# An attention block in fp32 on one core: the first chunk's transposes on TensorE, the local mask added on VectorE, and a new order of the first loads

## The chip, the core and the metric

The kernel runs on one core of a Trainium2 chip. The core has five engines that each work through a queue of their own in order: TensorE (PE; matmuls, and PEld, its weight loads), VectorE (DVE), ScalarE (ACT), GpSimd (POOL) and SyncE (SP, which here only issues transfers). The engines wait for each other by semaphores. Transfers between DRAM and the core's SBUF memory are issued from the queues of SP and ACT and carried out by 16 DMA engines. Matmuls write to PSUM, a small memory[...].

The metric is the device time of one execution in microseconds (us), lower is better.

## What is computed

The input x has 4 sequences of 1024 tokens with 512 features. After a layer norm (xn) two branches are added to x: an attention and a small product with an 8-bit rounding. The attention has 16 heads of 128 features:

```python
q  = apply_rope(rmsnorm(heads(xn @ Wq + bq), qn_w), pos)
lk = apply_rope(rmsnorm(heads(xn @ Wlk + blk), kn_w), pos)     # local keys
lv = heads(xn @ Wlv + blv)                                     # local values
# sparse part: groups of 4 tokens become one "entry" (softmax weights from xn @ Wcmp + bcmp)
entries = sum over 4 tokens of w_cmp * xn
ck, cv  = apply_rope(rmsnorm(entries @ Wk + bk, kn_w), ends), entries @ Wv + bv
sc = where(entry ended before the token, q . ck * scale, NEG); keep the 8 largest; softmax; times cv
# local part: windows of 128; a token sees the 128 tokens before it and itself
sl = where(0 <= distance <= 128, q . lk * scale, NEG); softmax; times lv
out = (sparse + local) * 0.5 @ Wo + bo
result = x + out + round8(xn * s) @ round8(input2 * s1) / (s * s1)
```

All of it is fp32, but for the 8-bit branch and some constants that are exact in bf16.

## The kernel before

**Tiles.** A chunk is 128 tokens (32 chunks, 8 to a sequence), a unit is one pair of heads of one chunk: 256 units, n = 8 x chunk + pair. All weights stay in SBUF: wqk_sb[u] (the pair's columns of Wq and Wlk, 1 MB), wlv_sb[u] (0.5 MB), wo_sb[u] (0.5 MB). wkv_sb holds Wk, Wv and the column of Wcmp.

**The loop** (L752) is a software pipeline over s from -2 to 257. In iteration s, in the order of the code, TensorE gets: scores of unit s, queries and keys of unit s+2 (`queries`), the output product of unit s-2 (`to_output`), the values of unit s+1 (`values_of`), and the weighted sum of unit s-1 (`values`). Between them `steps()` advances generators that prepare a chunk (`chunk_prep`: norm, transposes, entries) or do its 8-bit branch (`chunk_eight`). There is no planner: under `manual_schedule` each engine's queue has the order in which the code emits, and waits are put in for data and for buffers.

**A unit's way.** `queries` (L437) makes q and lk of both heads in one PSUM tile, qp. ScalarE sums squares (`square_sum`), GpSimd makes 1/rms (r), VectorE scales by it (`normalize`), VectorE and GpSimd rotate. q and k are then token by feature, and the scores need them feature by token. [...] `turn_keys` (L477) turns the blocks (two instructions into thb), SP writes them to DRAM in four transfers (qk), and `fetch_keys` (L497) reads them back in two (qT, lkT), in an order that completes the transpose.

**Scores** (`scores`, L537), for each head: a matmul of a bf16 identity with mask_b puts the local mask (0 or -1e30) into the PSUM columns of the window (L545), q with the previous chunk's keys and with its own adds to it (L547 and L554; a sequence's first chunk has no previous one, and a window of 128 columns), then q with the entries (L557) and a small mask for the last 32 of them (L558).

**Softmax.** `weigh` (L567): VectorE takes the negated maximum of the window (L579, a reduce), the 8 largest of the entries (L580) and replaces them by a mark (L583), ScalarE takes the exponentials with the sum (L584, L587). `settle` and `settle_window` divide by the sums; the result is prob.

**Weights.** They must be turned as well: `turn` (L621) in blocks on VectorE (L628), one write to DRAM (pr) and four reads back (`fetch`, L657; probT). The very last unit has no iteration behind it to hide that in, and uses `turn_last` (L639): TensorE transposes into PSUM (tiles of the tag pp), and one copy each on ScalarE and VectorE to probT.

**Buffers that matter:** PSUM tags qp (2 buffers), sc (2), pp (2, shared by values, transposes and the chunk generators), ctx and out (1 each); SBUF th, thb, probB and probT have one buffer each, lkT has ten.

**The start.** SP loads in this order: x of chunk 0, wqk_0, x of chunk 1, angles, wlv_0, Wk, Wv, Wcmp, wqk_1, angles, wlv_1, wqk_2, wlv_2. ScalarE's queue loads biases and small constants, and its first own work, the copy of chunk 0's transposed xn, stands behind those issues. Ahead of the loop the generator of chunk 0 runs up to "B3", which puts the entries' first matmuls (yp, L349) on TensorE ahead of the first queries. Later weights are loaded from ScalarE's queue at the ends of iterations -2 to 7 (L799 to L804).

Of the kernel before, what the change touches and what calls it, by code (L numbers as in the profile page):

```python
# [19 lines left out]
P = 128  # L20
D = 128
# [17 lines left out]
def kernel(  # L39
# [32 lines left out]
    NE = P // RATIO  # L72
    NT = B * NCH
    assert S // RATIO <= 2 * P and NU == 8 and HID == 512

# [59 lines left out]
    load_angles(0)  # L135
    load_wlv(0, nc.sync)

    wkv_sb = const.tile([P, KK, 2 * D + 1], F32, name="wkv_sb")
    nc.sync.dma_start(wkv_sb[:, :, 0:D], Wk.rearrange("(k p) n -> p k n", p=P))
    nc.sync.dma_start(wkv_sb[:, :, D : 2 * D], Wv.rearrange("(k p) n -> p k n", p=P))  # L140
    with nc.allow_non_contiguous_dma(reason="512 words once"):
        nc.sync.dma_start(
            wkv_sb[:, :, 2 * D : 2 * D + 1], Wcmp.rearrange("(k p) o -> p k o", p=P)
        )
    load_wqk(1, nc.sync)
# [4 lines left out]


    bias_f = work.tile([P, 1024], F32, tag="probT", name="bias_f", bufs=1)[0:BLK, 0:512]
    nc.vector.memset(bias_f, 0.0)
# [304 lines left out]
    def normalize(n):  # L458
# [16 lines left out]
        w["th"], w["thb"] = th, thb  # L475

    def turn_keys(n):  # L477

        w = units[n]
        th = w.pop("th").rearrange("p g (b i) -> p b g i", i=BLK)  # L480
        thb = w.pop("thb")

        nc.vector.transpose(
            thb[:, :, 0, :].rearrange("p b (i g) -> p b g i", g=2), th[:, :, 0:2, :]
        )
        nc.vector.transpose(
            thb[:, :, 1, :].rearrange("p b (g i) -> p b g i", g=2), th[:, :, 2:4, :]
        )
        turned = dram.tile([NB, NB, BLK, 4 * BLK], F32, tag="qk", name=f"qk_{n}")
        for a in range(NB):  # L490
            nc.sync.dma_start(  # L491
                turned[a].rearrange("b j x -> j b x"),
                thb[ds(a * BLK, BLK)].rearrange("p b t x -> p b (t x)"),
            )
        w["turned"] = turned

    def fetch_keys(n):  # L497
        w = units[n]
        turned = w.pop("turned").rearrange("a b j (t x) -> t (b j) a x", t=2)
        qT = work.tile([P, NB, 2 * BLK], F32, tag="qT", name=f"qT_{n}")  # L500
        lkT = work.tile([P, NB, 2 * BLK], F32, tag="lkT", name=f"lkT_{n}", bufs=NU + 2)
        nc.sync.dma_start(qT, turned[0])
        nc.sync.dma_start(lkT, turned[1])
        w["qT"], w["lkT"] = qT.rearrange("p a (i g) -> p (a i) g", g=2), lkT

# [31 lines left out]
    def scores(n, h):  # L537
# [6 lines left out]
        q = qT[:, :, h]  # L544
        nc.tensor.matmul(sc[:, loc], ident_b, mask_b[:, loc], start=True, stop=False)  # L545
        if c:
# [3 lines left out]
                units[n - NU]["lkT"][:, :, ds(h * BLK, BLK)],  # L550
                start=False,
                stop=False,
            )
        nc.tensor.matmul(  # L554
            blocks(sc[:, P : 2 * P]), q, lkT[:, :, ds(h * BLK, BLK)], start=False, stop=True
        )
# [10 lines left out]
    def weigh(n, h):  # L567
# [8 lines left out]
        if n % (NU * NCH) == 0:  # L576

            nc.gpsimd.memset(prob[:, 2 * P + NE : 4 * P], 0.0)
        nc.vector.reduce_max(neg[:, 0:1], sc[:, loc], AX.X, negate=True)  # L579
        nc.vector.max(top, sc[:, spa])  # L580
# [3 lines left out]
        nc.scalar.activation(  # L584
            prob[:, loc], sc[:, loc], AF.Exp, bias=neg[:, 0:1], accum_out=tot[:, 0:1]
        )
# [51 lines left out]

    def turn_last(n):  # L639

        parts = parts_of(n)
        g = len(parts)
        probT = work.tile([P, 1024], F32, tag="probT", name=f"probT_{n}", bufs=1)
        probT = of_heads(probT, n)
        for h in range(2):
            prob = heads.pop((n, h))["prob"]
            tp = pp(f"tp_{n}_{h}")
            for i in range(g):
                nc.tensor.transpose(tp[:, ts(i, P)], prob[:, ts(parts[i], P)], ident)
            copy = nc.vector.tensor_copy if h else nc.scalar.copy  # L650
            copy(
                probT[:, :, ds(h * g, g), :],
                tp[:, 0 : g * P].rearrange("p (g a i) -> p a g i", a=NB, i=BLK),
            )
        units[n]["probT"] = probT

# [67 lines left out]

    NN = NT * NU
    running = []
# [21 lines left out]
    pick_tokens()  # L748
    until(first, "B3")
    masks()  # L750

    for s in range(-2, NN + 2):  # L752
# [12 lines left out]
        for_unit(s, (weigh, 0), (weigh, 1))  # L765
        for_unit(s + 2, (queries,))
        for_unit(s, (settle, 0), (settle, 1))
        if s < 0:
            until(first, "A5" if s == -2 else "B6")
        steps()  # L770
        for_unit(s + 2, (squares, (0, 1, 2, 3)), (spread,))
        for_unit(s, (settle_window, 0), (settle_window, 1))
        for_unit(s - 2, (to_output,))
        steps()
        if s < NN - 1:
            for_unit(s, (turn,))
        if s == -1:
            until(first, "B7")
        for_unit(s + 1, (values_of,))
        if s == -1:  # L780
            until(first, "B8")
        for_unit(s + 2, (normalize,))
        for_unit(s - 1, (values,))
        if s < NN - 1:
            for_unit(s, (fetch,))
        else:
            for_unit(s, (turn_last,))
        for_unit(s + 2, (turn_keys,), (fetch_keys,))
        for_unit(s + 1, (keep_values,))
# [64 lines left out]
```

## Time and profile before

| | |
|---|---|
| Median of 3 runs | 2868.39 us (2865.25 to 2873.09) |
| The profiled execution | 2864.43 us, of which the traced span is 2862.7 us |
| TensorE busy | 2812.8 us (98%), 13417 matmuls |
| VectorE busy | 2209.7 us (77%) |
| ScalarE busy | 1300.8 us (45%) |
| GpSimd busy | 816.8 us (29%) |
| DMA | 408.25 MB, mean 143 GB/s |
| Granted TensorE clock, mean | 0.995 |

How to read it: a group's line gives the source line, engine, operation, output<-input by tile names, shapes and count; then busy time in us, the mean of one in ns, and the idle time of the engine ahead of it with what ended it. In the timeline a line is: start (us), duration (us), engine, line, operation, tiles, shape, how many were merged, and in brackets the idle time before it and its releaser. An fp32 matmul appears as two instructions (x2 for one product). Matmuls are pipelined, so that recorded durations overlap, and differences of starts tell how long one holds the engine. A row of the window table has: the window, its length, busy time and count for PE, PEld, DVE, ACT and POOL, then the granted clock, the DMA share and GB/s. The row of digits for PE is its busy share in tenths, in 40 equal slices of the span.

### The profile page before, as it was taken

To read this page: it belongs to the slowest core of one execution; us is meant where nothing else is said; L and a number is where in the kernel's file an instruction comes from. 1 tells how busy PE (TensorE), PEld (TensorE's weight loads), DVE (VectorE), ACT (ScalarE), POOL (GpSimd) and SP (SyncE) were. 2 spreads that over 40 slices of the span, in tenths; PEclk is the share of its full clock that TensorE was granted. 3 is DMA by queue.
4 is the path that set the end of the run, shared out by engine and by line. 5 is a ranking of instruction groups with operands and counts; after the bars stand their busy time and mean duration, and the time that the engine had idled before them with its cause. 6 is when DMAs were issued, how large, how long until landed. Compare 5 with 4: busy or idle time off the path is not lost. (4 is left out here: it accounts for less than half of the span.)

```text
span 2862.7 us, 48785 instructions
## 1 busy us (share of the span) xinstructions
PE 2812.8 (98%) x13417; PEld 1903.9 (67%) x13417; DVE 2209.7 (77%) x8636; ACT 1300.8 (45%) x5059; POOL 816.8 (29%) x1161
## 2 busy tenths in 40 slices
PE   6899999999999999999999999999999999999998
PEld 3566666666666666666666666666666666666766
DVE  5677778888777777788877777777887777787786
ACT  2344444444444444444444444444444444444443
POOL 3433222322233232222222332322223223322221
PEclk8999999999999999999999999999999999999999
DMA  7644445555444445555444444555554445455554
GB/s 240 169 138 134 130 136 151 149 151 144 137 124 132 136 133 143 147 150 150 145 132 124 138 131 131 152 147 146 146 150 126 131 126 139 131 151 148 145 146 123
DMA packets 639665, 408.25 MB, mean 143 GB/s; under 512 B 316480, under 2 KB 591776, under 8 KB 639392
## 3 DMA queue, kind: packets, MB, share of 16 engines
q1 hardware_dynamic: 627696, 391.57, 48.4%
q10 hardware_dynamic: 11696, 13.56, 1.5%
q8 instruction: 107, 1.75, 0.3%
q14 instruction: 166, 1.36, 0.2%
HBM read 216.72 MB, written 188.22 MB: 141 GB/s over the span
## 5 line engine op out<-in xcount | busy, mean ns | idle before, releaser
L442 PE MATMUL qp<-wqk,xnT 128*128 128x512 f32 x2048 | 947.5, 605 | 0.0
L442 PEld LDWEIGHTS qp<-wqk,xnT 128*128 128x128 f32 x2048 | 371.7, 192 | 381.3 <-issue 371.0
L584 ACT ACTIVATE prob<-sc,neg 128x256 f32<-128x256 f32 (+1 forms) x512 | 236.1, 461 | 626.5 <-DVE taken L583 601.1
L511 PEld LDWEIGHTS vp<-wlv,xnT 128*128 128x128 f32 x2048 | 389.0, 190 | 161.1 <-issue 112.7
L712 PE MATMUL op<-wo,cT 128*128 128x512 f32 x1024 | 488.0, 599 | 0.6 <-ACT cT L694 0.5
L511 PE MATMUL vp<-wlv,xnT 128*128 128x256 f32 x2048 | 483.8, 379 | 0.0
L628 DVE STREAM_TRANSPOSE probB<-prob 128x512 f32<-128x512 f32 (+2 forms) x510 | 289.1, 604 | 143.4 <-ACT prob L610 136.2
L293 ACT ACTIVATE junk<-qp 128x128 bf16<-128x128 f32 x1024 | 284.3, 278 | 247.8 <-PE qp L443 212.1
L523 ACT COPY lv<-vp 128x256 f32<-128x256 f32 x256 | 95.3, 372 | 515.0 <-PE cp L679 442.1
L306 POOL TENSOR_TENSOR rb<-th,cs 128x256 f32<-128x256 f32 x256 | 247.2, 966 | 279.3 <-DVE th L464 279.1
L287 POOL TENSOR_SCALAR r<-ss 128x4 f32<-128x4 f32 x256 | 49.5, 193 | 935.5 <-ACT junk L293 930.3
L712 PEld LDWEIGHTS op<-wo,cT 128*128 128x128 f32 x1024 | 186.6, 190 | 179.3 <-issue 128.9
L464 DVE SCALAR_TENSOR_TENSOR th<-qp,r,norm_w 128x128 f32<-128x128 f32 x1024 | 282.8, 338 | 27.4 <-POOL r L288 26.9
L679 PE MATMUL cp<-probT,lv 128*128 128x128 f32 x1920 | 297.9, 275 | 3.4 <-DMA probT<-pr 3.4
L679 PEld LDWEIGHTS cp<-probT,lv 128*128 128x128 f32 x1920 | 275.2, 192 | 18.2 <-issue 5.1
L288 POOL TENSOR_TENSOR r<-r,nhalf 128x4 f32<-128x4 f32 x256 | 259.7, 1014 | 21.4
L679 PE MATMUL cp<-probT,cv 128*128 128x128 f32 x1536 | 255.6, 275 | 0.0
L554 PE MATMUL sc<-lkT,qT 128*128 128x128 f32 x1024 | 210.7, 288 | 21.5 <-DMA lkT<-qk 21.4
L557 PE MATMUL sc<-ckT,qT 128*128 128x96 f32 (+7 forms) x1024 | 226.9, 303 | 0.0
L610 ACT ACTIVATE prob<-prob,tot 128x256 f32<-128x256 f32 (+1 forms) x512 | 222.8, 484 | 2.9 <-DVE tot L604 2.9
L679 PEld LDWEIGHTS cp<-probT,cv 128*128 128x128 f32 x1536 | 213.1, 192 | 0.0
L308 DVE TENSOR_TENSOR th<-thb,rb 128x128 f32<-128x128 f32 x256 | 87.2, 341 | 158.6 <-POOL rb L306 158.6
(120 smaller groups left out, 4143.1 us busy)
## 6 DMA issues: line engine op xcount, KB each, us to landing
qk<-thb SPq DMA_DIRECT2D x1024, 64.0 KB, 2.0
pr<-probB SPq DMA_DIRECT2D x127, 512.0 KB, 2.6
probT<-pr SPq DMA_DIRECT2D x508, 128.0 KB, 2.9
pr<-probB SPq DMA_DIRECT2D x96, 384.0 KB, 2.3
probT<-pr SPq DMA_DIRECT2D x384, 96.0 KB, 2.4
qT<-qk SPq DMA_DIRECT2D x256, 128.0 KB, 2.3
lkT<-qk SPq DMA_DIRECT2D x256, 128.0 KB, 2.5
x_norm<-_attn_hidden_states_dram SPq DMA_DIRECT2D x32, 256.0 KB, 3.2
```

The lines of the kernel that those rows point to most:

```text
L288: nc.gpsimd.tensor_tensor(r, r, nhalf[: ss.shape[0], 0:n], ALU.pow)
L293: nc.scalar.activation(junk[: src.shape[0]], src, AF.Square, accum_out=acc)
L306: nc.gpsimd.tensor_tensor(bb, x12, wide(cs[:, HALF:ROPE]), ALU.mult)
L442: nc.tensor.matmul(qp, xnT[:, k, :], wqk_sb[u][:, k, :], start=(k == 0), stop=False)
L464: nc.vector.scalar_tensor_tensor(th[:, i, :], qp[:, ts(i, D)], r[:, i : i + 1], norm_w[:, i // 2, :], ALU.mult, ALU.mult,)
L511: nc.tensor.matmul(vp[:, 0:256], xnT[:, k, :], wlv_sb[u][:, k, :], start=(k == 0), stop=(k == KK - 1),)
L557: nc.tensor.matmul(sc[:, spa], q, ckT[:, 0:m], start=True, stop=False)
L584: nc.scalar.activation(prob[:, loc], sc[:, loc], AF.Exp, bias=neg[:, 0:1], accum_out=tot[:, 0:1])
L610: nc.scalar.mul(prob[:, loc], prob[:, loc], tot[:, 0:1])
L628: nc.vector.transpose(pb[:, :, ds(h * g, g), :], prob[:, parts[0] * P : (parts[-1] + 1) * P].rearrange("p (g b i) -> p b g i", b=NB, i=BLK),)
L679: nc.tensor.matmul(blocks(cp[:, h, :]), v, probT[:, :, h * len(parts) + i - parts[0], :], start=(i == parts[0]), stop=(i == parts[-1]),)
L712: nc.tensor.matmul(op, cT[:, h, :], wo_sb[u][:, h, :], start=(u == 0 and h == 0), stop=(u == NU - 1 and h == 1),)
```

## The change

Three things are edited together.

1. **Transposes of the first chunk's units (n = 0 to 7) on TensorE.** `by_dma(n)` tells which units still take the way through DRAM: 8 to 254. For the others q and k are turned by four TensorE transposes into one pp tile (`turn_keys_here`, put behind the queries of the following unit) and copied by ScalarE (qT) and VectorE (lkT) in `keep_keys`. Their softmax weights are turned as in the old `turn_last`, now split into `turn_here` (transposes, put behind `values_of`) and `keep_turned` (the two copies, put where `fetch` stood). With two parts to a head (a first chunk) both heads share one pp tile. The last unit's weights take this way as before, but their transposes now stand ahead of `values` of the unit before.
2. **The local mask on VectorE.** The matmul L545 goes. In `weigh` the reduce is replaced by one fused instruction, which writes -(score + mask) back to the window's PSUM columns and returns their minimum, which is the negated maximum; the exponential then takes scale -1.
3. **The start.** wlv_0 is loaded after Wk and Wv, Wcmp from the head of ScalarE's queue in place of SP's. The generator of chunk 0 no longer runs to "B3" ahead of the loop: yp follows the first queries, and the entries' next matmul (ep) moves from iteration -2 to -1.

```diff
-    load_wlv(0, nc.sync)
     wkv_sb = const.tile([P, KK, 2 * D + 1], F32, name="wkv_sb")
     nc.sync.dma_start(wkv_sb[:, :, 0:D], Wk.rearrange("(k p) n -> p k n", p=P))
     nc.sync.dma_start(wkv_sb[:, :, D : 2 * D], Wv.rearrange("(k p) n -> p k n", p=P))
-        nc.sync.dma_start(wkv_sb[:, :, 2 * D : 2 * D + 1], Wcmp ...)
+    load_wlv(0, nc.sync)
...
+        nc.scalar.dma_start(wkv_sb[:, :, 2 * D : 2 * D + 1], Wcmp ...)
     bias_f = ...
...
+    def by_dma(n):
+        return NU <= n < NN - 1
+    def turn_keys_here(n):
+        w = units[n]
+        th = w.pop("th")
+        w.pop("thb")
+        w["tq"] = tq = pp(f"tq_{n}")
+        for i in range(4):
+            nc.tensor.transpose(tq[:, ts(i, P)], th[:, i, :], ident)
+    def keep_keys(n):
+        w = units[n]
+        tq = w.pop("tq").rearrange("p (t g a i) -> p t g a i", t=2, g=2, a=NB)
+        qT, lkT = key_tiles(n)
+        nc.scalar.copy(qT.rearrange("p a (i g) -> p g a i", g=2), tq[:, 0])
+        nc.vector.tensor_copy(lkT.rearrange("p a (g i) -> p g a i", g=2), tq[:, 1])
...
-        nc.tensor.matmul(sc[:, loc], ident_b, mask_b[:, loc], start=True, stop=False)
...
-        nc.vector.reduce_max(neg[:, 0:1], sc[:, loc], AX.X, negate=True)
+        nc.vector.tensor_tensor_reduce(
+            sc[:, loc], sc[:, loc], mask_b[:, loc], -1.0, TAKEN, ALU.add, ALU.min, neg[:, 0:1]
+        )
...
             prob[:, loc], sc[:, loc], AF.Exp, bias=neg[:, 0:1],
+            scale=-1.0,
             accum_out=tot[:, 0:1],
...
-    def turn_last(n):
+    def turn_here(n):
+        w, parts = units[n], parts_of(n)
         g = len(parts)
+        w["tp"] = []
+        for h in range(2):
+            prob = heads.pop((n, h))["prob"]
+            if h and g == 2:
+                tp = tp[:, g * P :]
+            else:
+                tp = pp(f"tp_{n}_{h}")
+            for i in range(g):
+                nc.tensor.transpose(tp[:, ts(i, P)], prob[:, ts(parts[i], P)], ident)
+            w["tp"].append(tp[:, 0 : g * P])
+    def keep_turned(n):
...
-    until(first, "B3")
     masks()
     for s in range(-2, NN + 2):
...
         for_unit(s + 2, (queries,))
+        if not by_dma(s + 1) and s < NU:
+            for_unit(s + 1, (turn_keys_here,))
         for_unit(s, (settle, 0), (settle, 1))
         if s < 0:
-            until(first, "A5" if s == -2 else "B6")
+            until(first, "B4" if s == -2 else "B6")
         steps()
         for_unit(s + 2, (squares, (0, 1, 2, 3)), (spread,))
+        if not by_dma(s + 1) and s < NU:
+            for_unit(s + 1, (keep_keys,))
         for_unit(s, (settle_window, 0), (settle_window, 1))
...
-        if s < NN - 1:
-            for_unit(s, (turn,))
+        if by_dma(s):
+            turn(s)
...
         for_unit(s + 1, (values_of,))
+        if not by_dma(s):
+            for_unit(s, (turn_here,))
         for_unit(s + 2, (normalize,))
         for_unit(s - 1, (values,))
-        if s < NN - 1:
-            for_unit(s, (fetch,))
+        if by_dma(s):
+            fetch(s)
         else:
-            for_unit(s, (turn_last,))
-        for_unit(s + 2, (turn_keys,), (fetch_keys,))
+            for_unit(s, (keep_turned,))
+        if s + 2 >= NU:
+            for_unit(s + 2, (turn_keys,), (fetch_keys,))
```

## The prediction

> **What bounds the kernel now.** I read the page first, then the stretches by window, then one unit in the timeline, then the list of waits. The page gives TensorE 98% of the span and a row of nines; the window table shows where the other 2% is:
>
> ```profile
> PE 2812.8 (98%) x13417; PEld 1903.9 (67%) x13417; DVE 2209.7 (77%) x8636; ACT 1300.8 (45%) x5059; POOL 816.8 (29%) x1161
> PE   6899999999999999999999999999999999999998
> 0.00:40.00 40.00, 18.78 (x56) 11.39 (x57) 16.99 (x64) 6.46 (x25) 9.74 (x30) 0.91 0.76 224
> 40.00:80.00 40.00, 27.76 (x107) 17.46 (x105) 25.82 (x98) 12.04 (x56) 16.01 (x19) 0.84 0.84 257
> 80.00:120.00 40.00, 34.82 (x145) 21.68 (x146) 27.86 (x121) 15.47 (x68) 21.46 (x25) 0.90 0.61 173
> 120.00:160.00 40.00, 39.83 (x187) 26.27 (x186) 27.98 (x124) 17.94 (x74) 9.42 (x14) 1.00 0.51 142
> ```
>
> So there are two kernels: the first 120 us, where TensorE is idle for 38.6 us (120 - 18.78 - 27.76 - 34.82) and its granted clock (the column after POOL) falls to 0.84 to 0.91; and 2,740 us in which it never stops. What it waits for in the first part is in the timeline, first at the loads, then at the keys on their way through DRAM:
>
> ```profile
> 15.41 3.76 PE L349 MATMUL yp<-wkv_sb,xnT 128*128 128x257 f32 x8 [8.00 <-DMA wkv_sb<-in_L_attn_Wcmp_dram]
> 38.47 6.08 PE L442 MATMUL qp<-wqk,xnT 128*128 128x512 f32 x8
> 52.56 0.77 PE L554 MATMUL sc<-lkT,qT 128*128 128x128 f32 x2 [5.57 <-DMA lkT<-qk]
> 82.45 0.79 PE L554 MATMUL sc<-lkT,qT 128*128 128x128 f32 x2 [7.64 <-DMA lkT<-qk]
> ```
>
> Eight queries matmuls take 6.08 us there and 3.68 us later: after a long wait TensorE also runs slow. In the steady part the order of starts tells what an instruction really costs; durations overlap and don't:
>
> ```profile
> 1599.78 0.61 PE L679 MATMUL cp<-probT,lv 128*128 128x128 f32 x4
> 1600.45 0.27 PE L545 MATMUL sc<-mask_b,ident_b 128*128 128x256 bf16 x1
> 1600.56 0.40 PE L547 MATMUL sc<-lkT,qT 128*128 128x128 f32 x2
> 1600.79 0.40 PE L554 MATMUL sc<-lkT,qT 128*128 128x128 f32 x2
> 1601.21 0.18 PE L558 MATMUL sc<-mask_b,ident_b 128*128 128x32 bf16 x1
> 1601.24 0.27 PE L545 MATMUL sc<-mask_b,ident_b 128*128 128x256 bf16 x1
> 1601.35 0.40 PE L547 MATMUL sc<-lkT,qT 128*128 128x128 f32 x2
> 1602.00 0.18 PE L558 MATMUL sc<-mask_b,ident_b 128*128 128x32 bf16 x1
> 1602.03 3.68 PE L442 MATMUL qp<-wqk,xnT 128*128 128x512 f32 x8
> 1605.55 0.38 PE L443 MATMUL qp<-bias_b,sel 128*128 128x512 bf16 x1
> 1605.76 1.88 PE L712 MATMUL op<-wo,cT 128*128 128x512 f32 x4
> ```
>
> The mask matmul L545 holds TensorE 0.11 us (1600.45 to 1600.56), L558 0.03. Vector's side:
>
> ```profile
> L579 DVE TENSOR_REDUCE neg<-sc 128x1 f32<-128x256 f32 x448 | 180.0, 402 | 8.8 <-PE sc L558 8.4
> L721 DVE TENSOR_TENSOR x_sum<-x_sum,op 128x512 f32<-128x512 f32 x32 | 22.0, 688 | 62.4 <-PE op L712 62.4
> L594 DVE DVE_READ_ACCUMULATOR prob<-taken,prob 128x1 f32 x512 | 42.4, 83 | 0.0
> ```
>
> [...] after L558 (0.03 us) the eight L442 take 3.52 us, not 8 x 0.43 = 3.44 as four L712 (1.72 us) would have it, so 0.08 + 0.03 = 0.11 us of fp32 weight load lie open behind the short matmul. [...] here four L339 transposes, warm, take 0.44 us in all (44.60 to 45.04), so I use 0.11 each. [...]
>
> **The mask off TensorE, 256 units.** For each head L545 goes. First head of a unit: it stood behind a 0.11 us matmul (L679), which will hide the next weight load just as well: 0.11 us saved. Second head: it stood behind L558 and covered the 0.11 us load of the query weights; without it the load starts at L558 and only L558's 0.03 us covers it. Saved: 0.03. Together 0.14 us a unit (0.137 with unrounded starts), whether the mask had 256 or 128 columns. Bounds: 0.06 if the first head's load is exposed too, 0.22 if none is. Units 8 to 255: 248 x 0.137 = 34.0 us.
>
> **The mask on Vector, 512 instructions.** The fused add, negate and minimum reads PSUM and SBUF, writes PSUM and reads out an accumulator; the trace has no such row. Below: the plain reduce's 0.40. Nearest row: L721 less 256 elements at 1.03 ns (L579's 402 at 256 against 270 at 128) is 0.42, the three-operand L427 (750) is 0.49 in the same way, plus 0.08 for the accumulator: 0.50 to 0.57. Above: 1.0, if the unknown form takes two passes. I take 0.57, that is 0.35 us more a unit. What hides it: Vector works 8.6 us of a unit's 11 (2209.7/256), and the turning of the weights (L628) waits for ScalarE's L610 (136.2 us in all, 0.53 a unit), which is behind the squares of this iteration's queries and not behind Vector; a further wait of 0.3 us for r follows it in chunks without earlier window. Without that cover it would delay the next keys by 0.35 a unit.
>
> **What is late next.** Keys of unit n leave in iteration n-2 and must land by n. From the last query matmul to the landing of lkT takes 14.7 us in a first chunk of a sequence (1512.05 to 1526.8), and two units less the 4.8 us of scores and queries leave 2 x 9.9 - 4.8 = 15.0: the 0.3 to spare is what two shorter units take (0.27), and landings vary by more. I count none of the 0.137 there: 24 units of sequences 2 to 4 give back 3.3 us. In second chunks I find lkT landing -0.5 to 2.4 us ahead of the scores, half under 0.3: half of 32 x 0.137, 2.2 us, is given back. Later chunks have 1 to 3 us ahead; 1.9 us for scattered waits. Kept: 34.0 - 7.4 = 26.6 us.
>
> **First chunk and start.** Added: eight transposes a unit, 8 x 0.11 = 0.87 us of TensorE, and two ScalarE and two Vector copies of about 0.4 (L523: 372 ns). Removed: Vector's four block transposes (1.6 us), all of SP's issues for q, k and weights (1 + 4 + 4 + 2 a unit), the wait for the keys. Loads: Wcmp's issue (0.51) moves from SP to the head of ScalarE's queue, where eleven issues and the first copy (ended 10.05) stand behind it: that copy moves to 10.5, and the queue's biases land behind its 512 small packets (bias_b was ready at 11.5, its first use moves to 15.6). wlv (0.5 MB) moves behind Wk and Wv. The entries' first matmuls move behind queries(0).
> Ends of scores, before: 38.5, 54.4, 64.8, 84.3, 95.9, 106.9, 118.1, 127.9 for units 0 to 7. After, step by step: queries(0) from 10.5, wqk_0 having landed at 7.1, half of them at the slow clock: 15.9. Entries' matmuls 1.7: 17.7. queries(1), whose weights land at about 18: 21.8. ScalarE copies y and takes its exponentials first, so squares(0) starts at 19.5, and norm and rotation end 5.65 us later as before: 25.15. TensorE waits 3.4 us for them, turns the keys: 25.7. Entries: ep 26.1, kv 26.9, squares 27.7, unit 1's squares 29.3, GpSimd's r 30.6 (ahead of the entries' rotation in its queue), rotation 31.0, ckT 32.0, scores(0) end 32.8. queries(2), slow clock again as before, 6.1: 38.9; turned keys, one more transpose group and values, 41.5; weights turned once ScalarE's L610 has passed, 42.45; scores(1) end 43.4. From then on a unit is TensorE's own sum: scores 0.92, queries 3.73, keys 0.44, output 1.72, values 1.73, weights 0.44, context 0.89 = 9.87, plus the chunk work of an iteration (0.55, 0.86, 0.17): 53.3, 63.2, 73.6, 83.5, 94.2, 104.3. ScalarE's and Vector's halves end within that (ScalarE's L610 at 6.7 us of the unit, weights are turned at 7.6). At unit 7: 127.9 - 104.3 = 23.6, less 0.3 for its own weights: 23.3 us gained, with 15 to 26 as bounds (a wait of 1 us a unit for copies or PSUM tiles; no clock loss).
> **The end.** The last unit already turned its weights on TensorE; they now stand ahead of values(254), which waited for DRAM until 2848.0: 0 within 0.5.
>
> **The sum.** 26.6 + 23.3 = 50 us. The profiled execution took 2864.43 us (span 2862.7): 2814. The median of the runs lies 4 us above it: 2818.
>
> **The rivals.** (1) As above, 2806 to 2829: chance 0.56. (2) The keys' way through DRAM takes more: in all chunks up to the fourth nothing is kept, and each later unit half: steady gain 8, total 31, 2837. For it: landings 0 to 1 us ahead are common; against: chunks 4 to 8 show 1 to 3. 0.17. (3) The first chunk trades DRAM for waits on PSUM copies and ScalarE's weight-load issues (four a unit, 0.5 each); a wait of 2 us a unit leaves 8 of the 23: 2833. Against: ScalarE's 9.7 us wait at unit 0 was for keys' DMAs, which go. 0.12. (4) Both loads stay hidden and nothing is given back: 0.22 x 248 + 23 = 78, or 34 + 23 = 57 with the second head's exposed: 2790 to 2811. 0.07. (5) Slower: the fused instruction makes Vector the bound. Vector has about 1.6 us a unit to spare (10.9 less 8.6 and 0.6 for GpSimd's rb) and the 50 us are another 0.2; past 1.8 us a unit, 0.9 a head, 1.3 us an instruction, the kernel is slower; at 1.5 us it adds 2.2 a unit, 0.4 too much, 256 x 0.4 = 102 us: 2970. Against: nothing of 256 fp32 elements takes over 0.5 us on Vector. 0.05. (6) No change within 0.3% (2860 to 2877): 0.03.
>
> **How the numbers follow.** 0.3% (8.6 us) is about what a measurement of this kernel can tell from no change. Cases 1 to 4 are faster, 0.92; same 0.03; slower 0.05. The time is case 1's. The range reaches from 2804 (half of case 4) to 2840, which takes in 2 and 3; it leaves out 0.12.
>
> **What would show it.** Right: no L545 rows; the scores' first head starting straight behind L679 and 0.11 between L558 and the second head's first product's effective start (0.03 by starts, the next pitch longer by 0.08); a fused Vector row under 0.6 us with an accumulator read; unit 7's scores at 104 us; units of later chunks 0.14 shorter, those of first chunks not. Wrong: waits of TensorE for lkT of over 15 us in all beyond the first chunk; Vector over 90% busy; waits for tq or tp in the first chunk; scores(0) later than 36 us.

## The result

The changed kernel takes 2828.1 us (median of 2824.1 to 2831.7), the kernel before, run beside it, 2868.5: a ratio of 0.986 with an interval of 0.984 to 0.988. The forecast was 2818 in a range of 2804 to 2840, so it lies inside, 10 us above the forecast. The profiled execution took 2828.88 us with a span of 2827.2, against a span of 2862.7 before: 35.5 us less where the sum had 50. The medians differ by 40.4; single runs of one kernel differ by 8 us here and by 13 in a later comparison, so everything below is read from stages of the traces.

The page of the changed kernel, its engines and TensorE's row of slices, and then its first four stretches in the window table (busy time and instructions of TensorE, its weight loads, VectorE, ScalarE and GpSimd, then the granted clock, the DMA engines' share and GB/s):

```profile
PE 2775.0 (98%) x12770; PEld 1879.6 (66%) x12969; DVE 2277.4 (81%) x9132; ACT 1302.9 (46%) x5075; POOL 818.0 (29%) x1161
PE   7999999999999999999999999999999999999998
0.00:40.00 40.00, 24.32 (x69) 13.13 (x71) 16.40 (x64) 7.49 (x30) 9.76 (x30) 0.91 0.75 226
40.00:80.00 40.00, 34.67 (x150) 23.20 (x149) 31.68 (x125) 17.83 (x78) 22.64 (x26) 0.93 0.62 209
80.00:120.00 40.00, 39.71 (x181) 25.52 (x183) 28.90 (x136) 18.73 (x83) 17.34 (x23) 0.99 0.25 73
120.00:160.00 40.00, 39.84 (x191) 27.75 (x193) 29.64 (x135) 18.99 (x74) 9.26 (x14) 1.00 0.43 119
```

TensorE's idle time in the first 120 us fell from 38.6 to 21.3 us (120 - 24.32 - 34.67 - 39.71), and the clock of the second and third stretch rose from 0.84 and 0.90 to 0.93 and 0.99. (Some 200 matmul records are missing from this trace, none of them of the queries, so units are measured by the start of their first query matmul.) What is left of the waits stands in the timeline of TensorE:

```profile
10.86 6.34 PE L443 MATMUL qp<-wqk,xnT 128*128 128x512 f32 x8 [3.09 <-DMA scales<-in_L_ffn_scale_dram]
20.17 3.67 PE L443 MATMUL qp<-wqk,xnT 128*128 128x512 f32 x8 [1.02 <-DMA wqk<-in_L_attn_Wlk_dram]
27.30 1.09 PE L488 MATMUL tq<-ident,th 128*128 128x128 f32 x4 [3.24 <-DVE th L310]
42.65 2.98 PE L535 MATMUL vp<-wlv,xnT 128*128 128x256 f32 x8 [2.10 <-DVE lkT L495]
54.34 1.99 PE L535 MATMUL vp<-wlv,xnT 128*128 128x256 f32 x8 [0.78 <-DVE lkT L495]
77.47 3.66 PE L535 MATMUL vp<-wlv,xnT 128*128 128x256 f32 x8 [2.40 <-DVE total L384]
```

(The 3.09 us at 10.86 ended with ScalarE's copy of xnT, which ran from 10.22 to 10.81, and not with the small load that the line names.) No wait for keys from DRAM is left here (14 waits for lkT, 21.4 us in all, had been in the list of the kernel before; 8 with 3.9 us are in this one, all later). In their place the values' matmuls L535 wait for a PSUM tile: the tag pp has two, and where a chunk generator takes a tile between tq and vp (xp, yp and ep in these three units), vp gets the one that the turned keys tq lay in, which is free once VectorE has copied lkT. At 77.43 that copy ended (it began at 77.01); "total L384", which the line names, stood right behind it. After the waits of 2.10 and 2.40 us TensorE also runs slow: 2.98 and 3.66 us where eight L535 take 1.89 in a steady unit, and the granted clock is 0.50 from 43.51 to 46.92 us and from 77.64 to 81.06. After the wait of 0.78 us it does not (1.99 us, a granted clock of 1.00). The length of a wait alone doesn't decide it: after one of 2.01 us in another kernel, keys_act_tail at 2807.16 us, four L718 take 0.68 us and the next four 0.61, where four take 1.06 in the changed kernel while its granted clock is 0.50, from 2812.61 on.

The steady part, in the timeline of TensorE where the kernel before was shown:

```profile
1603.49 0.39 PE L718 MATMUL cp<-probT,cv 128*128 128x128 f32 x2
1603.72 0.40 PE L570 MATMUL sc<-lkT,qT 128*128 128x128 f32 x2
1603.95 0.40 PE L577 MATMUL sc<-lkT,qT 128*128 128x128 f32 x2
1604.19 0.37 PE L580 MATMUL sc<-ckT,qT 128*128 128x96 f32 x2
1604.40 0.18 PE L581 MATMUL sc<-mask_b,ident_b 128*128 128x32 bf16 x1
1604.43 0.48 PE L570 MATMUL sc<-lkT,qT 128*128 128x128 f32 x2
1604.74 0.40 PE L577 MATMUL sc<-lkT,qT 128*128 128x128 f32 x2
```

The first head starts straight behind the values. Behind L581 the second head's L570 starts 0.03 us later, lasts 0.48 instead of 0.40, and the next start follows after 0.31 instead of 0.23. The record of its weight load (PEld) begins at 1604.40, 0.03 us ahead of it, the first head's at 1603.61, 0.11 ahead: this is the weight load laid open, 0.08 us, as forecast. VectorE's new rows, in the groups by form (count, busy us, mean ns of one, idle time ahead):

```profile
L603 DVE CUSTOM_DVE_ANT_0 sc<-sc,mask_b 128x256 f32<-128x256 f32 x448 | 184.3, 411 | 2.5 <-PE sc L581 2.5
L603 DVE DVE_READ_ACCUMULATOR2_ANT neg<- 128x1 f32 x512 | 70.3, 137 | 0.0
```

From the fused instruction's start to that of the next operation it is 0.48 to 0.52 us (median 0.51 of 448), against 0.31 to 0.34 (median 0.33) for the plain maximum: 0.36 us more a unit, where 0.35 was forecast.

By place, from the query starts of both traces: units 0 to 9 gained 13.2 us, units 10 to the last query 24.8, and from there to TensorE's last instruction 2.1 were lost: 35.9 (the span is 35.5 shorter).

### The profile page after: what moved, and what is told of

Its sections match the earlier page's. It is cut to its first block, busy times and chain, and to the rows that moved or that the text cites. A ratio compares the mean times of both kernels' runs of the same rounds, so it can differ in the third digit from the quotient of the medians.

```text
span 2827.2 us, 48528 instructions
## 1 busy us (share of the span) xinstructions
PE 2775.0 (98%) x12770; PEld 1879.6 (66%) x12969; DVE 2277.4 (81%) x9132; ACT 1302.9 (46%) x5075; POOL 818.0 (29%) x1161
## 5 line engine op out<-in xcount | busy, mean ns | idle before, releaser
L535 PEld LDWEIGHTS vp<-wlv,xnT 128*128 128x128 f32 x2048 | 391.1, 191 | 170.4 <-issue 109.5
L535 PE MATMUL vp<-wlv,xnT 128*128 128x256 f32 x2048 | 488.6, 382 | 6.2 <-DVE lkT L495 2.9
L659 DVE STREAM_TRANSPOSE probB<-prob 128x512 f32<-128x512 f32 (+2 forms) x494 | 282.9, 610 | 79.4 <-ACT prob L641 75.8
L718 PE MATMUL cp<-probT,lv 128*128 128x128 f32 x1920 | 298.3, 275 | 0.7 <-DMA probT<-pr 0.7
L718 PEld LDWEIGHTS cp<-probT,lv 128*128 128x128 f32 x1920 | 275.3, 192 | 14.3 <-PE vp L535 1.1
L289 POOL TENSOR_TENSOR r<-r,nhalf 128x4 f32<-128x4 f32 x256 | 259.9, 1015 | 21.4
L718 PE MATMUL cp<-probT,cv 128*128 128x128 f32 x1536 | 255.6, 275 | 0.0
L580 PE MATMUL sc<-ckT,qT 128*128 128x96 f32 (+7 forms) x1024 | 226.2, 303 | 0.0
L309 DVE TENSOR_TENSOR th<-thb,rb 128x128 f32<-128x128 f32 x256 | 87.1, 340 | 158.9 <-POOL rb L307 158.9
L718 PEld LDWEIGHTS cp<-probT,cv 128*128 128x128 f32 x1536 | 213.2, 192 | 0.0
```

Source lines behind the costliest of these rows:

```text
L289: nc.gpsimd.tensor_tensor(r, r, nhalf[: ss.shape[0], 0:n], ALU.pow)
L535: nc.tensor.matmul(vp[:, 0:256], xnT[:, k, :], wlv_sb[u][:, k, :], start=(k == 0), stop=(k == KK - 1),)
L580: nc.tensor.matmul(sc[:, spa], q, ckT[:, 0:m], start=True, stop=False)
L659: nc.vector.transpose(pb[:, :, ds(h * g, g), :], prob[:, parts[0] * P : (parts[-1] + 1) * P].rearrange("p (g b i) -> p b g i", b=NB, i=BLK),)
L718: nc.tensor.matmul(blocks(cp[:, h, :]), v, probT[:, :, h * len(parts) + i - parts[0], :], start=(i == parts[0]), stop=(i == parts[-1]),)
```

## Experiments

**One part at a time.** Four kernels made from the kernel before. The first has only the mask's part of the change:

```diff
-        nc.tensor.matmul(sc[:, loc], ident_b, mask_b[:, loc], start=True, stop=False)
-        nc.vector.reduce_max(neg[:, 0:1], sc[:, loc], AX.X, negate=True)
+        nc.vector.tensor_tensor_reduce(sc[:, loc], sc[:, loc], mask_b[:, loc], -1.0, TAKEN, ALU.add, ALU.min, neg[:, 0:1])
```

> The kernel before with the mask alone moved (L545's two matmuls a unit out, the fused instruction on VectorE in). Theory: TensorE gains 0.137 us a unit in the steady units (0.11 at the first head, 0.03 at the second, where the query weights' load is laid open), nothing in the first chunk, where units wait for keys from DRAM, and 7 to 9 us of 34 are given back to later landings: 26 us less, 2842 us. Rival, both weight loads hidden: units shorter by 0.22 us, 45 us less or more. Rival, VectorE's 0.33 us more a unit isn't covered: 0 us or slower, with TensorE waiting for lkT or qT by over 20 us in all.

2847.9 us, ratio 0.992 (0.990 to 0.994): 17.6 us less, where the theory had 26. The median unit is shorter by 0.136 us at every one of the eight places of a chunk in its sequence: the price of L545 is right to the third digit, and neither rival's (0.22, 0) occurs. Units 10 to the last query gain 21.4 of the 33.7 possible, and the first chunk, still waiting for keys from DRAM, loses 5.5 us, where the theory had nothing. The list of TensorE's waits has more of them; the kernel before, then this one:

```profile
PE sc L554 <- DMA lkT<-qk: 21.4, 14, 7.6
PE sc L553 <- DMA lkT<-qk: 29.8, 16, 7.9
```

The second kernel keeps VectorE's plain maximum and leaves the mask's matmuls out:

```diff
-        nc.tensor.matmul(sc[:, loc], ident_b, mask_b[:, loc], start=True, stop=False)
```

> The kernel before with L545's matmuls left out and VectorE's plain maximum kept: the local causal mask is left out of the computation, so this prices TensorE's part alone. Theory (VectorE's fused instruction is hidden): the same per-unit gain as with the mask moved, 0.137 us, and the same total within 3 us (26 us less). Rival (part of what is given back is VectorE's): 5 to 9 us shorter than with the mask moved, 31 to 35 us less than before. Both say what remains is the keys' way through DRAM.

2838.1 us, ratio 0.989 (0.988 to 0.991): 27.4 us less, 9.8 less than with the mask moved. So the rival holds nearly in its size (5 to 9; its total, 31 to 35 less, was not reached): the fused instruction isn't free in the kernel before, though with four runs of each kernel the intervals touch. Where it costs can be told only roughly, from the two traces: 3.4 us in the first chunk, 2.9 in units 10 to the last query (24.3 against 21.4), 3 at the end. The third and fourth kernels:

```diff
+            for_unit(s + 1, (turn_keys_here,))
...
+            for_unit(s + 1, (keep_keys,))
...
+            for_unit(s, (turn_here,))
...
+            for_unit(s, (keep_turned,))
```

> The kernel before with the first chunk's queries, keys and weights turned on TensorE and nothing else. Theory, as the trace of the changed kernel now has it (unit 7's scores end at 114.7 us, 13.2 earlier than before): most of that is the turning, so unit 7's scores end at 113 to 118 here and the run is 10 to 15 us shorter, 2855; waits of values' PSUM tile for the copies of turned keys, with a slower clock behind them, stay as they are there. Rival: the new order of loads and of the entries is what opens the start and the turning alone gains under 6 us. My own forecast, 23.3 us for turning and order together without waits for PSUM tiles, would have unit 7 at about 105 to 108.

```diff
-    load_wlv(0, nc.sync)
...
+    load_wlv(0, nc.sync)
...
+        nc.scalar.dma_start(wkv_sb[:, :, 2 * D : 2 * D + 1], Wcmp ...)
...
-    until(first, "B3")
-            until(first, "A5" if s == -2 else "B6")
+            until(first, "B4" if s == -2 else "B6")
```

> The kernel before with the order of the loads and of the entries' steps changed and nothing else (keys still through DRAM). Theory: unit 0's scores wait for keys from DRAM whose way takes as long as before, and queries(0) starts no earlier (10.9 in the changed kernel), so scores of unit 0 end within 1.5 us of 38.5 and the run changes by under 3 us either way. Rival: Wcmp at the head of ScalarE's queue delays ScalarE's first copy and with it everything: unit 0 later by 1.5 us and more. Rival: the order gains 3 to 6 us by itself.

Turning alone: 2850.4 us, ratio 0.994 (0.992 to 0.995), 15.1 less; unit 7's scores end at 116.8, 11.1 earlier than before. The order alone: 2863.9, ratio 0.999 (0.9985 to 1.000), nothing, as the first theory had it, though not for the reason that it gave: queries(0) does start earlier, at 10.9 instead of 19.0, but unit 0's scores end only 1.4 us earlier, and unit 7's at 129.0 instead of 127.9. In the list of TensorE's waits of the kernel that only turns, the keys' waits are gone and the PSUM tile's are there:

```profile
PE vp L535 <- DVE lkT L495: 3.3, 3, 1.6
PE vp L535 <- DVE total L384: 2.1, 1, 2.1
PE sc L578 <- DMA lkT<-qk: 1.7, 4, 0.7
```

The three parts alone sum to 17.6 + 15.1 + 1.6 = 34.3 us, the whole change gives 37 to 40. The mask's loss of 5.5 us arose in a first chunk that waits for DRAM, and the changed kernel's doesn't; that this is the difference is likely, but no run separates it. With the keys turned on TensorE, unit 7's scores end 2.1 us earlier than by turning alone (114.7 for 116.8), which takes in the order of loads and the mask together.

How much the steady part moves by itself is seen here too: with nothing changed in units 10 to 255, the order alone loses 1.0 us there and the turning alone gains 2.4, both by other landings.

**How much VectorE has to spare.** The changed kernel with one more maximum for each head:

```diff
+        nc.vector.reduce_max(neg[:, 1:2], sc[:, loc], AX.X, negate=True)
         nc.vector.max(top, sc[:, spa])
```

> The changed kernel with one more maximum over the local scores for each head on VectorE, its result unused (0.32 us a head, 0.65 a unit; VectorE from 8.9 to 9.5 us of a unit's 11). Theory (VectorE's work is mostly covered, but some waits for keys from DRAM start with it): the plain maximum against the fused instruction, 0.33 us a unit, was worth about 3 us in units 8 to 255, so twice as much work costs 5 to 15 us, 2833 to 2843, in scattered waits for lkT and qT in first and second chunks; chunks 4 to 8 of a sequence keep their time. Rival (VectorE is at its bound): 0.65 us in each of 248 units, 160 us, 2990. Rival (wholly hidden): within 3 us of the changed kernel.

2937.4 us, slower than the kernel before by 2.5% (1.023 to 1.027), and 109 us more than the changed kernel. Neither my theory's 5 to 15 nor the full 160: of 0.65 us a unit, 166 us in all, some 100 come out (2928.4 - 2827.2 by spans). VectorE's list of waits says why; first of the kernel before, its three longest but for rb, then of the changed kernel, then of this one (us in total, times, longest):

```profile
DVE probB L628 <- ACT prob L610: 136.2, 144, 1.9
DVE logits L360 <- ACT y L358: 77.4, 32, 7.7
DVE x_sum L721 <- PE op L712: 62.4, 32, 5.7
```

```profile
DVE th L309 <- POOL rb L307: 158.9, 256, 0.6
DVE probB L659 <- ACT prob L641: 75.8, 128, 1.4
DVE logits L361 <- ACT y L359: 57.9, 31, 6.4
DVE x_sum L760 <- PE op L751: 45.8, 32, 6.5
DVE th L465 <- POOL r L289: 44.9, 77, 2.4
```

```profile
DVE th L309 <- POOL rb L307: 158.2, 256, 0.6
DVE th L465 <- POOL r L289: 58.1, 80, 2.3
DVE logits L361 <- ACT y L359: 51.7, 31, 6.5
DVE probB L660 <- ACT prob L642: 51.6, 102, 1.2
DVE x_sum L761 <- PE op L752: 12.7, 7, 6.5
```

The wait for rb is one of 0.62 us in each unit, inside VectorE's own chain, and is as long in all three kernels. The others (with those for fp and for scores) come to 346 us in the kernel before, 230 in the changed one and 177 here, and are not lower in the next kernel that overloads VectorE (179, with the entry mask there). From 346 to 230 are 0.45 us a unit, about the fused instruction's 0.36 and TensorE's 0.14. So only what lies above some 177 was room: 53 us, 0.2 us a unit, in the changed kernel, not the 230 of its list and not the 1.5 us a unit that its idle time without the rb wait (2827.2 - 2277.4 - 158.9 = 390.9) would come to. Busy and idle time say the same: of 158 us more work here, 56 came out of VectorE's idle time, and the span grew by 101. What gives is the keys: from the last query matmul to the keys' turning it is a median of 7.4 to 7.9 us over the places of a chunk in the kernel before, 8.0 to 8.5 in the changed one, 8.9 to 10.4 here; keys landed 0.4 to 2.2 us before their scores, then 0.4 to 1.6, and here -0.1 to 0.2. TensorE waits for qT and lkT 54 us in all, where the changed kernel has 6:

```profile
PE sc L570 <- DMA qT<-qk: 33.6, 32, 2.3
PE sc L577 <- DMA lkT<-qk: 20.2, 45, 1.3
```

By the starts of its matmuls it is more. Against keys_act_tail below, which has the changed kernel's steady part and no record missing, 54 us more pass ahead of the first product of scores and 38 between products with local keys: 92 of the 107 us between the two. And the place where VectorE's lateness enters is ScalarE's squares, which stand behind exponentials that wait for VectorE's maxima. The first square begins a median of 0.5 us after the last query matmul in the kernel before and in the changed one, and 2.1 us here; r comes 5.4 us after it instead of 3.6.

**The open weight load.** The entry masks of both heads side by side, behind both heads' products:

```diff
+        for_unit(s, (mask_entries, 0), (mask_entries, 1))
```

> The changed kernel with the two heads' entry mask matmuls (L581) put side by side behind both heads' products. Theory of the prediction (a weight load of fp32 queries, 0.11 us, lies open behind a matmul of 0.03): the opening between the heads goes, the one ahead of the next queries stays, so each unit is 0.08 us shorter, 256 x 0.08 = 20 us less before anything is given back, 13 to 20 kept: 2808 to 2815. Rival (the longer second head has another cause, such as the change of tile): 0 within 4 us. VectorE's start for the first head is up to 0.8 us later, which the cover of ScalarE's wait should hide.

2822.4 us, ratio to the kernel before 0.985 (0.984 to 0.987). The median unit is shorter by 0.005, 0.031, 0.057, 0.083 and then four times 0.093 us from the first to the last chunk of a sequence, that is by 0.026 for every 32 entries that the product ahead of the second head has more. So the load is hidden as far as the matmul ahead is long, and the forecast's 0.08 a unit is right for a product of 128 entries, too high for shorter ones. The timeline of TensorE shows it for 128 entries: no longer L570 behind L580, and 0.24 to the next start.

```profile
1685.12 0.40 PE L580 MATMUL sc<-ckT,qT 128*128 128x128 f32 x2
1685.35 0.40 PE L570 MATMUL sc<-lkT,qT 128*128 128x128 f32 x2
1685.59 0.40 PE L577 MATMUL sc<-lkT,qT 128*128 128x128 f32 x2
```

Of 17 us in medians of units (20 forecast) 9.3 are kept to the last query (13 to 20 forecast), and some are lost again behind it: the span is 7.0 us shorter. Against the changed kernel the intervals overlap, so this one can't be called faster by the runs.

Then the entry mask too on VectorE:

```diff
-        nc.tensor.matmul(sc[:, ds(2 * P + m - NE, NE)], ident_b, mask_b[:, 2 * P : 2 * P + NE], start=False, stop=True)
+        nc.vector.tensor_tensor(last, last, mask_b[:, 2 * P : 2 * P + NE], ALU.add)
```

> The changed kernel with the entry mask also off TensorE: no L581, a VectorE addition of 32 columns for each head in its place (about 0.2 us by L608 and L634, 0.4 to 0.5 a unit). Theory: each unit is shorter by two starts of 0.03 and two opened weight loads of 0.08, 0.22 us, 56 us before anything is given back; VectorE's 0.45 us and landings from DRAM take back 15 to 30: 2787 to 2802. Rival (VectorE's part eats it): 2815 and over. Rival (the entries' product of 32 columns is too short to hide a load of 0.11 us): nothing gained in first chunks of a sequence, 0.22 in later ones.

2894.8 us, 1.010 (1.009 to 1.012) of the kernel before. Undisturbed units are shorter by 0.06, 0.11, 0.16, 0.22 and 0.23, as the lengths of the products say (the third theory, with the second head's opening as well), but the addition (200 ns each) is past VectorE's 0.2 us, and keys land late: 47 us of waits for qT and lkT. The forecast of 2787 to 2802 missed by 100 us on the same error as above.

**The PSUM tile, and the end.** Both copies of turned keys on ScalarE; the last unit's turning behind the values before it:

```diff
-        nc.vector.tensor_copy(lkT.rearrange(...), tq[:, 1])
+        nc.scalar.copy(lkT.rearrange(...), tq[:, 1])
...
+        if s == NN - 1:
+            turn_here(s)
```

> The changed kernel with two edits, which the trace tells apart by place: in the first chunk both copies of turned keys are ScalarE's, and in the last unit the weights are turned behind the values of the unit before, as in the kernel before. Theory (the values' PSUM tile waits for VectorE's copy of lkT, which stands behind work that GpSimd stretches, and the slower clock comes from that wait): the waits of 2.1, 0.8 and 2.4 us of vp go and unit 3 is 3 to 4.5 us shorter, the first chunk 5 to 8; unit 7's scores end at 107 to 110 instead of 114.7. Rival (the wait only moves, to squares behind the second copy or to the exponentials): under 2 us. Tail: from the last scores' end to the end 14.5 to 15 us instead of 16.0. Both together 5 to 9 us, 2820.

2826.1 us, 0.987 (0.985 to 0.988): no different. In the timeline the wait of 2.40 us is down to 0.36, the scores that follow it, unit 4's, end at 79.8 instead of 83.2, and then ScalarE is late with the weights of unit 4:

```profile
74.65 1.99 PE L535 MATMUL vp<-wlv,xnT 128*128 128x256 f32 x8 [0.36 <-ACT lkT L495]
89.64 0.97 PE L682 MATMUL tp<-ident,prob 128*128 128x128 f32 x4 [2.06 <-ACT prob L641]
```

Unit 7's scores end at 114.5, where 114.7 was: the wait moved, as the rival said. What it moved to is VectorE. ScalarE's second copy holds it 0.26 us here (88.91 to 89.17), but its exponentials had waited for VectorE until 84.89 us; in the changed kernel that was 85.64, although here the scores end 3.4 us earlier:

```profile
84.89 0.37 ACT L610 ACTIVATE prob<-sc,neg 128x128 f32<-128x128 f32 x1 [3.81 <-DVE taken L609]
85.64 0.37 ACT L610 ACTIVATE prob<-sc,neg 128x128 f32<-128x128 f32 x1 [1.50 <-DVE taken L609]
```

(The first line is this kernel's, the second the changed one's.) VectorE's normalization of unit 5's keys, which stands ahead of those maxima, began at 79.57 in this kernel and at 79.85 in the changed one, both after a wait for GpSimd's r (2.19 and 1.86 us). The squares for r were done at 74.05 here, but GpSimd began it at 78.24, right behind a part of the 8-bit branch (L266, 76.89 to 78.16) that had waited for VectorE in turn. So in the first chunk VectorE and GpSimd with the 8-bit branch come next, close behind the PSUM tile.

From the last scores to the end of TensorE it takes 13.7 us, against 16.1 in the changed kernel; but the kernel that only turns has the changed kernel's order there and takes 14.0, so the order isn't the cause. The clock is most of it. In the changed kernel it is 0.50 from 2811.72 to 2815.13 us, and the matmuls there are slow, which in the other two they are not:

```profile
2811.71 1.11 PE L682 MATMUL tp<-ident,prob 128*128 128x128 f32 x4 [0.42 <-ACT prob L641]
2812.61 1.06 PE L718 MATMUL cp<-probT,lv 128*128 128x128 f32 x4
```

The kernel that only turns has 0.66 and 0.61 us for the same two, keys_act_tail 1.04 for all eight L682 and 0.61 for four L718. In the kernel that only turns it takes 3.4 us from these transposes to the output product behind them, where the changed kernel takes 5.0. The remaining 0.4 us lie ahead of the first transpose, where VectorE has the fused instruction. Why one ran slow and the other did not (waits of 1.70 and 0.42 us ahead of it, and 1.29 and 0.42) stays open.

**Giving VectorE room by order.** Four kernels that move VectorE's work into its waits. First, the first head's weights are scaled ahead of the squares and turned right behind the settling:

```diff
         for_unit(s, (settle, 0), (settle, 1))
+        if by_dma(s):
+            settle_window(s, 0)
+            turn_head(s, 0)
```

> The changed kernel, where weights go through DRAM, with the first head's scaling by ScalarE (L641) ahead of the squares and the first head's turning by VectorE (L659, 0.5 us) straight behind the settling, while VectorE waits for the second head's scaling anyway. Theory (VectorE is within 0.3 us a unit of its bound because it works in a loop with a wait for L641 in it, and keys leave late by what it is late): keys are turned 0.3 to 0.5 us earlier after their queries (8.3 us in the changed kernel, 7.8 in the kernel before), the 8.8 us given back in units 10 to 255 fall to 3 to 6: 2822 to 2826. Rival (the squares are later by the scaling, r with them, and keys leave no earlier): no change within 2 us.

2842.7 us, 0.992 (0.990 to 0.993): 14.6 us slower than the changed kernel. Both theories failed. VectorE works 2288 us, 11 more than in the changed kernel, but its waits moved:

```profile
DVE th L465 <- POOL r L289: 144.1, 216, 2.4
DVE probB L659 <- ACT prob L641: 38.5, 67, 1.1
```

ScalarE's squares now stand behind a scaling that waits for VectorE's settling as well; r is later whenever VectorE is late, and VectorE then waits for r. From the last query matmul to the first square it is a median of 1.6 us (0.5 in the changed kernel), to the end of r 5.0 (3.6), and keys are turned 0.5 to 1.2 us later. A chain that TensorE's queries paced had become a loop over VectorE, ScalarE and GpSimd.

The same with the masks side by side, and with the entry mask on VectorE, both with the last unit's order:

```diff
+            settle_window(s, 0)
+            turn_head(s, 0)
...
+        for_unit(s, (mask_entries, 0), (mask_entries, 1))
```

> Early turning of the first head, entry masks side by side, and the last unit's weights turned behind the values of the unit before. Theory: the side-by-side masks shorten units by 0, 0.03, 0.06, 0.08 and four times 0.09 us over the chunks of a sequence, 0.067 on average, 17 us, of which 9 were kept without the early turning; with the slack that it gives 13 to 17 are kept, and the last unit gives 1.5: 2828 less 4, 15 and 1.5, 2804 to 2811. Rival (keys' way through DRAM takes it all the same): 2816 to 2820.

and, with VectorE's addition of the entry mask in the place of the last line,

> Early turning, the entry mask added by VectorE (0.48 us a unit more there), and the last unit's order. Theory (half a microsecond of VectorE's work moved into its wait pays for the half added): VectorE is where it was in the changed kernel, and TensorE's 0.055, 0.11, 0.16, 0.22 and four times 0.23 a unit, 0.18 on average, 46 us, comes out for the most part: 2785 to 2805. Rival (VectorE's sum of work decides, not where its wait stands): still 2850 and over, as without the early turning (2895) less some us.

2853.5 (0.995, 0.994 to 0.997) and 2957.2 us (1.032, 1.030 to 1.033): 31 and 62 us slower than without the early turning, and outside every forecast. Last, the weights' turning (turn(s), called as `between`) behind the start of the next keys' rotation, and SP's order of keys and weights exchanged:

```diff
         nc.vector.tensor_tensor(a, x12, wide(cs[:, 0:HALF]), ALU.mult)
+        if between:
+            between()
...
+            for_unit(s + 2, (turn_keys,))
         if by_dma(s):
             fetch(s)
...
-            for_unit(s + 2, (turn_keys,), (fetch_keys,))
+            for_unit(s + 2, (fetch_keys,))
```

> Where weights go through DRAM, VectorE's turning of the weights (1.03 us) stands behind the normalization of the next keys, in VectorE's wait of 0.62 us for GpSimd's half of the rotation, and SP issues the keys' writes ahead of the weights' fetch; entry masks side by side and the last unit's order as before. Theory (what limits VectorE is a loop: maxima, ScalarE's exponentials, its squares, GpSimd's r, normalization and turning of keys, next maxima, 10.3 us with the turning of weights waiting in it for L641, against TensorE's 10.3 to 11.4 a unit): the loop is 0.5 us shorter, keys are turned at 8 us or less after their queries with the side-by-side masks (8.2 to 9.1 without), units keep their 0.03 to 0.09, TensorE waits for qT and lkT under 5 us (10.6 with the side-by-side masks alone): 2822 less 1.9 for the end less 6 to 10, 2810 to 2815. Rival (weights, turned 1.9 us later and fetched behind the keys, take their 3.9 us of slack at the values, and TensorE waits for probT): over 10 us of waits for probT, 2820 to 2835. Rival (VectorE's sum of work decides): keys turned no earlier, 2818 to 2822.

2858.8 us, 0.997 (0.996 to 0.998). The first rival holds in kind, not in size (it had 2820 to 2835). The wait for rb went, and its time came back as one for r; the keys' landings gained (0.6 us of waits for lkT are left), and the weights, fetched last, lost more. VectorE's list, then TensorE's:

```profile
DVE th L467 <- POOL r L289: 303.9, 219, 2.4
DVE th L311 <- POOL rb L307: 6.2, 10, 0.6
```

```profile
PE cp L723 <- DMA probT<-pr: 45.1, 54, 2.7
```

The weights' landing was 3.9 us ahead of the values in the changed kernel (median) and is 0.9 here.

## Why the prediction was right, and where it was off

- **The mask off TensorE: right.** 0.137 us a unit forecast, 0.136 measured in three kernels. The weight load behind the short L581 was seen in the starts (the whole load of 0.11 us, of which 0.08 lies open, was my estimate from the starts of the kernel before; from 1603.61 to 1604.98 us of this trace the loads of the other fp32 matmuls of the scores begin 0.10 to 0.11 us ahead of them) and, made to go away, gave 0.093 us at most.
- **What is given back: right in size, 7.4 forecast, 8.9 measured** (33.7 possible in units 10 to 255, 24.8 kept). Of first chunks of sequences 2 to 4, 1.1 of 3.3 us were kept, of second chunks 1.7 of 4.4, and the rest was scattered. But kernels that don't differ there do so by 1 to 4 us (24.8 kept here, 28.8 with ScalarE's copies in the first chunk), so the single terms weren't measured, and part of the agreement is luck.
- **The fused instruction: its price right (0.35 forecast, 0.36 measured), its cover wrongly sized.** "VectorE has about 1.6 us a unit to spare" came from busy time and the rb wait; the runs show about 0.66 in the kernel before (346 less 177 us over 256 units, an estimate) and 0.2 after. The reading that failed is that VectorE's wait for ScalarE's scaling is "not behind Vector": the squares ahead of that scaling follow VectorE's maxima as soon as VectorE is late. Rival (5) was set at 1.3 us an instruction; one maximum more, 0.8 us a head with the fused instruction, already made the kernel 2.5% slower than before. The forecast held because the fused instruction's 0.36 and TensorE's 0.14 stayed within the 0.66; that the error cost so little is luck.
- **First chunk and start: the term that was mis-sized.** 23.3 us forecast, 13.2 measured, below its own bounds of 15 to 26. Scores' ends were forecast at 32.8, 43.4, 53.3, 63.2, 73.6, 83.5, 94.2 and 104.3; they came at 35.8, 47.5, 58.4, 68.3, 83.2, 93.1, 104.2 and 114.7. Three of the 10.4 us were missing at unit 0 (queries(0) took 6.34 us, where 5.4 were forecast and queries(1) took 3.67, with a granted clock of 1.00 in the profile for both; and the second unit's weights landed at 20.0 where "about 18" was assumed); 2.1 came in units 1 and 2, where vp waited 2.10 and 0.78 us for the copy of lkT and, after the first of them, ran slow; and 4.5 in unit 4's line of the list, 83.2 for 73.6, of which 2.4 are the same wait and 1.8 the slow clock after it. The step that failed is "from then on a unit is TensorE's own sum": copies were only checked for being shorter than a unit, not for the PSUM tile that they hold, and no loss of clock was counted. This is rival (3)'s mechanism, with 6.6 us of the 15 that it priced. The price of 0.11 us for a transpose held: four of tq take from 39.52 to 39.95. With the copy taken from VectorE the chunk was no shorter, because VectorE and GpSimd with the 8-bit branch came next.
- **The order of loads: it adds nothing by itself**, as one kernel shows; with the turning, it and the mask together gave 2.1 us at unit 7. The prediction had put the two into one sum.
- **The end: forecast 0 within 0.5, measured 2.1 lost.** Of these, 0.9 us lie ahead of the last scores' end (TensorE waits 1.41 us for their qT, where the kernel before had 0.58 for qT and 0.49 for lkT) and 1.3 behind it, where the changed kernel lost 1.6 us in its slow stretch. The kernel before had one there too (a granted clock of 0.50 from 2849.07 to 2852.48), so the 1.3 aren't split further.
- **Why only 10 us off in the result:** 26.6 and 23.3 were forecast, 24.8 and 13.2 came, and 2.1 went at the end, so the profiled execution gained 14 us less than the sum of 50. The medians of this comparison lie 4.9 us further apart than the two profiled executions; that part is chance.

## What to carry to other kernels

An engine's room isn't one minus its busy share, and it isn't the sum of its waits either: here VectorE was all but full at 81% busy with 230 us of waits outside its own chain, of which 53 gave way. A kernel with a known bit of work added to the engine measures the room; ask too what in its waits follows the engine itself by way of another. When an edit moves work off the bound engine, price what it uncovers as well as what it removes (here a product of 160 entries hid 0.09 us of the next fp32 weight load that one of 0.03 us left open). And before turning a wait on a transfer into copies out of PSUM, count who takes the tile next: with two tiles of a tag, the copy's place in its queue was on the path in three of the eight units.

## What the runs showed that was not expected

- The hidden part of an fp32 weight load grew with the matmul ahead of it: with the entry masks side by side the median unit was shorter by 0.026 us more for every 32 columns up to 128, and by 0.093 at most.
- Two small VectorE operations, begun just after a GpSimd operation of 512 columns, ended only when it did: L625 (32 columns, at 72.06 us) took 1.10 us and L634 (2 columns, at 74.01) 1.21, where they take 0.18 and 0.17 otherwise; GpSimd's rounding of w2 ran from 71.84 to 73.11 and from 73.94 to 75.21. VectorE waited for nothing from there to the copy of lkT, so these two, 1.96 us longer than otherwise, account for most of the 2.40 us that the vp at 77.47 waited. It happened in four units, and not behind every such GpSimd operation (the one before, from 70.50 to 71.76, stretched nothing); why isn't shown.
- Moving 0.5 us of VectorE's work forward into a wait cost 14.6 us, because it put a wait for VectorE ahead of ScalarE's squares.
